# Layer 0's feed-forward in float32r halves, its transposes three tiles later, and row statistics a quad ahead

## The chip, the cores and the metric

The kernel runs on one core of a Trainium2 chip. The core has a matrix engine (PE, or TensorE) that writes into the accumulator memory PSUM, and three engines for elementwise work: DVE (VectorE), ACT (ScalarE) and POOL (GpSimd). SP only issues transfers. Each engine works through its own queue in order and waits on semaphores for the others. POOL cannot read PSUM. The metric is device time in microseconds for one execution; lower is better. An execution under the profiler gives the trace that the views below are read from.

## What is computed

The input is `x`, 8 batches of 512 rows of 256 values. Two transformer layers follow; every sub-layer normalizes its rows first and adds its result to `x`.

```python
x = x + attention0(layernorm(x))     # 16 heads of 16, causal; gamma, beta
x = x + ffn0(layernorm(x))
x = x + attention1(layernorm(x))     # 16 heads of 16, causal within 64 rows; biases, Wo
x = x + ffn1(layernorm(x))           # 256 -> 768 -> 256, int32 weights times 1/127

def fp4_linear(x, w):                # blocks of 16 along the last axis, both operands
    return fp4_quant_dequant(x) @ fp4_quant_dequant(w).T

def ffn0(y):                         # 256 -> 704 -> 256
    h = silu(fp4_linear(y, w_gate)) * fp4_linear(y, w_up)
    return fp4_linear(h, w_down)
```

`fp4_quant_dequant` divides each block of 16 by a sixth of its largest magnitude, rounds to the grid 0, 0.5, 1, 1.5, 2, 3, 4, 6 and multiplies back. So `h` has to be quantized row by row between the two matrix products of layer 0's feed-forward.

## The kernel before

The kernel has four stages, and each fills the whole core: attention 0, feed-forward 0, attention 1, feed-forward 1. A tile framework gives each tile a place and semaphores, and orders each engine's instructions by a plan made ahead; instructions that are pinned (`pin`, `keep_in_program_order`) keep the order of the code. The line numbers are those of the kernel before.

**Attention** (both layers, `attention`, L331) works in quads: four heads of one batch, two quads to a unit, 32 quads in all. `body` (L693) runs through the quads; in each it computes the maxima of the quad after next (`scores`, L436), the exponentials of this one (`Outputs`, L532) and the sums of the last one, in positions 0 to 5 (0 to 3 in layer 1), and hangs side work on these positions with `at`. Side work for batch `c + 2` is: `norm` (row statistics on DVE and POOL, then four normalizations on ACT, L742), `turned` (transposes on PE, L739), and the projections `load_q`, `load_k` (L744), whose pieces go through `store` (POOL, then SP to HBM) and come back by `fetch`. The masks are added on PE by a product of an identity (`ident_b`, bf16) with a mask that holds -1e30. `VP` holds the values of an even and an odd batch.

During attention 0 a generator, `before_ffn` (L863), is advanced at three of ten steps: it quantizes the weights of feed-forward 0 and prepares batch 0 for it. The row statistics for the other batches of feed-forward 0 also run in this stage, where the plan finds room.

**Feed-forward 0** (L976 to L1086) takes 32 row tiles of 128 rows. For tile n the code emits: `gated` (L1019), two halves of 352 columns; each half is four float32 products (gate and up, two blocks of 128 of the contraction) into one pair of PSUM banks, then SiLU on ACT (L1031) and the product with `up` on DVE (L1032) into the row tile `h`. Then quantization of `h` (`quantize`, L197): block maxima on DVE (L217), scale and reciprocal (L223 to L225), a product on POOL (L226), a magnitude on ACT (L274), two rounding steps on DVE (L276, L278), and the product with the scale on POOL (L279). Two tiles later `down` (L1034) transposes `h` in six pieces on PE (`ph`, L1041; five of 128 columns and one of 64), copies them to `hT` with three ACT copies (L1045 to L1048), and multiplies with the weights in six float32 products (`pd`, L1052). DVE adds the result to `x` (L1056). Each batch's input is prepared one batch ahead by `prepare` (L1011): normalize, quantize, transpose (`pt_f`, L853), copy to `fyT` (L858). `late_weights` (L984) brings in the weights of layer 1, and from the 27th tile on the opening of attention 1 (L666) is advanced between the tiles.

**Feed-forward 1** (L1099) already works with halves. A float32 tensor is split into `hi`, its value rounded to float32r, and `lo`, the remainder; products of float32r tiles replace one float32 product.

## Time and profile before

| What | us |
|---|---|
| Median of 3 runs (lowest 1334.25, highest 1334.98) | 1334.26 |
| The profiled execution | 1330.82 |
| Its span, first to last instruction | 1329.1 |

The stages, from the view of busy time by stretch (us):

| Stage | stretch | length | PE | DVE | ACT | POOL |
|---|---|---|---|---|---|---|
| Attention 0 | 0 to 485.6 | 485.6 | 403.2 | 387.9 | 279.7 | 249.1 |
| Feed-forward 0 | 485.6 to 807.1 | 321.5 | 300.5 | 217.1 | 113.6 | 133.1 |
| Attention 1 | 807.1 to 1171.7 | 364.6 | 335.4 | 247.0 | 176.7 | 237.9 |
| Feed-forward 1 | 1171.7 to 1329.1 | 157.4 | 146.7 | 77.9 | 80.8 | 68.5 |

A row of the timeline gives the start, the length, the engine, the line of the code, the operation, output and inputs by the program's names, the shapes, a count of merged instructions, and in brackets the idle time before it with what ended that. PEld is the loading of weights into PE, which overlaps the products. Lengths of PE rows overlap their successors, so a pace is read from start to start. A row of waits names the waiting engine and line, whom it waited for, the sum in us, the number of times and the longest. A TensorE clock of 1.00 is full speed.

### The profile page before, as it was taken

What the parts mean: (1) busy time and instruction counts of PE and PEld (TensorE: products, weight loads), DVE (VectorE), ACT (ScalarE), POOL (GpSimd) and SP (SyncE); (2) the same over time, 40 slices, a digit from 0 to 9 for tenths busy, and PEclk for the clock granted to TensorE, in tenths of its full rate; (3) what the DMA queues carried; (4) which work ended last, traced back from release to release, by engine and by line L of the source; (5) the groups of instructions that cost most, each with busy time, mean ns of one, the idle gap of its engine ahead of it and who ended that gap; (6) DMA issues with size and microseconds to landing.
All of it is one profiled execution on the core that took longest, in us unless ns stands there. A gap on an engine that the chain in (4) does not pass through costs nothing. (4 is left out here: it accounts for less than half of the span.)

```text
span 1329.1 us, 23108 instructions
## 1 busy us (share of the span) xinstructions
PE 1185.7 (89%) x8815; PEld 791.4 (60%) x8846; DVE 929.9 (70%) x1657; ACT 650.8 (49%) x1057; POOL 688.7 (52%) x912
## 2 busy tenths in 40 slices
PE   4678889889978998998999998999999999889998
PEld 2444454445534455665666666676767667668887
DVE  4699989796699847686766657676667767545553
ACT  3265655566665663332333323544455444555553
POOL 4266556464456334443443544766667566634443
PEclk9899999899989998999999999999999999999999
DMA  7643334354433310000000044454543535000001
GB/s 219 142 103 75 87 80 91 83 111 87 96 68 97 60 33 1 24 24 0 1 1 0 0 111 93 96 123 84 113 103 91 125 80 128 7 0 33 25 33 42
DMA packets 50448, 92.07 MB, mean 69 GB/s; under 512 B 6428, under 2 KB 43420, under 8 KB 44188
## 3 DMA queue, kind: packets, MB, share of 16 engines
q1 hardware_dynamic: 49452, 89.74, 29.6%
q8 instruction: 72, 1.18, 0.4%
q10 hardware_dynamic: 816, 0.79, 0.2%
q14 instruction: 44, 0.36, 0.1%
q0 software_dynamic: 64, 0.00, 0.0%
HBM read 61.15 MB, written 29.36 MB: 68 GB/s over the span
## 5 line engine op out<-in xcount | busy, mean ns | idle before, releaser
L134 POOL TENSOR_SCALAR_AFFINE_SELECT ex<-ex 128x256 f32<-128x256 f32 (+2 forms) x512 | 263.4, 525 | 230.3 <-ACT ex L575 129.9
L575 ACT ACTIVATE ex<-t 128x1024 f32<-128x1024 f32 (+1 forms) x192 | 168.0, 882 | 121.1 <-PE t L564 110.7
L469 DVE TENSOR_REDUCE mx<-s 128x2 f32<-128x1024 f32 (+2 forms) x192 | 196.6, 1035 | 39.9 <-PE s L458 30.6
L605 ACT ACTIVATE ex<-t 128x640 f32<-128x640 f32 (+1 forms) x128 | 96.8, 757 | 123.4 <-PE t L595 108.6
L635 PE MATMUL po<-ex,vp 128*32 128x128 f32 (+4 forms) x2816 | 142.9, 322 | 3.1 <-POOL ex L134 2.0
L488 DVE TENSOR_REDUCE mx<-s 128x4 f32<-128x768 f32 x128 | 121.3, 953 | 31.9 <-PE s L482 30.9
L1052 PE MATMUL pd<-wd,hT 128*128 128x256 f32 (+1 forms) x384 | 101.3, 407 | 15.9 <-ACT hT L1045 15.1
L635 PEld LDWEIGHTS po<-ex,vp 128*32 128x32 f32 x2816 | 71.2, 109 | 60.5 <-issue 31.2
L1103 POOL TENSOR_TENSOR hT<-gh,hT 128x512 fp32r<-128x512 f32 x48 | 61.7, 1291 | 82.6 <-ACT hT L1102 66.1
L453 PE MATMUL s<-kk_both,qq_both 96*128 96x512 bf16 (+3 forms) x352 | 81.9, 314 | 19.0 <-DVE mx L469 8.8
L1052 PEld LDWEIGHTS pd<-wd,hT 128*128 128x128 f32 (+1 forms) x384 | 70.1, 195 | 47.9 <-ACT hT L1045 28.0
L279 POOL TENSOR_TENSOR h<-mg_h,sc_h 128x704 f32<-128x704 bf16 x32 | 45.4, 1420 | 97.6 <-DVE mg_h L278 90.3
L1026 PE MATMUL gu<-wg,fyT 128*128 128x352 f32 x256 | 93.9, 470 | 0.0
L1026 PE MATMUL gu<-wu,fyT 128*128 128x352 f32 x256 | 86.3, 459 | 0.0
L475 PE MATMUL s<-wmask,ident_b 128*128 128x384 bf16 x256 | 83.6, 332 | 1.4 <-DVE mx L488 1.4
L564 PE MATMUL t<-qq_both,kk_both 108*128 108x512 bf16 (+3 forms) x352 | 70.4, 304 | 12.1 <-DVE mx L469 6.1
L226 POOL TENSOR_TENSOR xn_h<-h,rc_h 128x704 f32<-128x704 f32 x32 | 45.0, 1405 | 61.1 <-DVE rc_h L225 57.5
L458 PE MATMUL s<-cmask,ident_b 128*128 128x128 bf16 (+1 forms) x321 | 76.4, 238 | 0.0
L1170 DVE SCALAR_TENSOR_TENSOR gh<-ggu,gsl 128x512 f32<-128x512 f32 x48 | 33.2, 691 | 55.6 <-ACT gsl L1168 55.1
L1031 ACT ACTIVATE sl<-gu 128x352 f32<-128x352 f32 x64 | 29.4, 460 | 75.8 <-PE gu L1026 75.6
L1026 PEld LDWEIGHTS gu<-wu,fyT 128*128 128x128 f32 x256 | 48.6, 190 | 27.4 <-issue 1.0
L453 PEld LDWEIGHTS <-qq_both 96*128 96x128 bf16 x352 | 32.6, 101 | 51.5 <-issue 29.6
(256 smaller groups left out, 2661.1 us busy)
## 6 DMA issues: line engine op xcount, KB each, us to landing
q_hbm<-qp SPq DMA_DIRECT2D x96, 128.0 KB
k_hbm<-kp SPq DMA_DIRECT2D x96, 128.0 KB
qq_both<-q_hbm SPq DMA_DIRECT2D x44, 256.0 KB
kk_both<-k_hbm SPq DMA_DIRECT2D x22, 384.0 KB
qq_both<-q_hbm SPq DMA_DIRECT2D x44, 128.0 KB
kk_both<-k_hbm SPq DMA_DIRECT2D x22, 256.0 KB
qq<-q_hbm SPq DMA_DIRECT2D x20, 256.0 KB
out_dram<-go SPq DMA_DIRECT2D x16, 256.0 KB
```

Source lines behind the costliest of these rows:

```text
L134: nc.gpsimd.affine_select(out=t, in_=t, compare_op=ALU.is_ge, fill=0.0, base=base, pattern=[[0, n] for n in shape[1:-1]] + [[sign, shape[- ...
L453: pin(nc.tensor.matmul(bank[:, a * w : (a + 1) * w], lhsT=q[:KF, hs[j], t * P : w], rhs=k[:KF, hs[j], :w], start=(a == 0), stop=False, ski ...
L458: pin(nc.tensor.matmul(bank.rearrange("p (i k) -> p i k", k=w)[:, :, t * P :], lhsT=ident_b, rhs=cmask[:, : len(part), :], start=False, st ...
L469: nc.vector.tensor_reduce(dst, src, AX.X, ALU.max)
L475: pin(nc.tensor.matmul(sc[:, a, : 2 * BAND], lhsT=ident_b, rhs=mask.rearrange("p a k -> p (a k)"), start=True, stop=False,))
L488: nc.vector.tensor_reduce(mx[:, t2 : t2 + 2, js[0] : js[0] + 2].rearrange("p t j -> p j t"), sc[:, :, : 2 * BAND].rearrange("p j (t k) -> ...
L564: pin(nc.tensor.matmul(bank[:, a * w : (a + 1) * w], lhsT=k[: KF + 12, self.hs[j], t * P : (t + 1) * P], rhs=q[: KF + 12, self.hs[j], t * ...
L575: nc.scalar.activation(ex[:, :banks, :used], sc[:, :banks, :used], AF.Exp, scale=QSCALE)
L605: nc.scalar.activation(by_head[:, :, :w], sc[:, :, :w], AF.Exp, scale=QSCALE)
L635: pin(nc.tensor.matmul(self.o[HP * j : HP * (j + 1), t * P : t * P + w], lhsT=vp[:, kt, 4 * c + j, :], rhs=self.ex[kt, j][:, x0 : x0 + w], ...
L1026: nc.tensor.matmul(gu[:, i, :352], lhsT=YT[b][:, e, t * P : (t + 1) * P], rhs=w[:, e, f], start=(e == 0), stop=(e == NE - 1),)
L1052: nc.tensor.matmul(pd[:, :D], lhsT=hT[:n, k, :], rhs=wd1[:n, k, :], start=(k == 0), stop=(k == NH - 1),)
```

## The change

- *Float32r halves in feed-forward 0.* `wg1`, `wu1` and batch 0's rows are split into `HALVES` at the end of `before_ffn`; `wd1` is split where feed-forward 0 begins (one ACT copy and one POOL subtraction of 1536 columns); the rows of later batches by `split` when they are transposed (two ACT copies out of PSUM, one POOL subtraction). Each float32 product becomes three float32r products: high by high, high by low, low by high (`PAIRS`).
- *128 rows throughout.* `h` and `wd1` are padded with zeros from 704 to 768, so the sixth piece has 128 rows as the others.
- *Transposes three tiles later.* `turn_rows` transposes tile n - 3 at the head of step n, into one pair of banks, with one ACT copy for the high half and one DVE subtraction for the low half (768 columns each); `down` follows after `gated`. There is one pair of `hT` and there are four fixed row tiles `h`.
- *Quantization.* The scale uses a sixth rounded up, so the reciprocal is no longer multiplied by `DOWN` (L225 goes); the inexact form works in place, and its second rounding writes float32.
- *Statistics.* In both attentions the row statistics of batch `c + 2` move from a quad's first position in `r == 1` to the last position of `r == 0`, and the normalizations go one tile to a position.
- *Places.* The bf16 identity goes: the masks hold +1e30 and are added through the negated identity. `cmask` and the second `VP` live in the attention's own pool, and `VP` 1 is cleared in each attention. The opening of attention 1 keeps the pieces of a unit's q and k in one slot, that of `wd1`, and has one buffer for the remainder.

The diff, cut to its core:

```diff
         if not exact:
-            nc.vector.tensor_scalar(sc, am, sixth, 1e-12, ALU.mult, ALU.max)
+            nc.vector.tensor_scalar(sc, am, SIXTH_UP, 1e-12, ALU.mult, ALU.max)
             nc.vector.reciprocal(rc, sc)
-            nc.vector.tensor_scalar(rc, rc, DOWN, None, ALU.mult)
-            nc.gpsimd.tensor_tensor(blocks(xn), src, wide(rc), ALU.mult)
+            nc.gpsimd.tensor_tensor(src, src, wide(rc), ALU.mult)
...
-            nc.vector.scalar_tensor_tensor(mg, mg, MAGIC, xn, ALU.max, ALU.subtract)
-        nc.gpsimd.tensor_tensor(dst, blocks(mg), wide(sc), ALU.mult)
+            nc.vector.scalar_tensor_tensor(xn, mg, MAGIC, xn, ALU.max, ALU.subtract)
+        nc.gpsimd.tensor_tensor(dst, blocks(mg) if exact else dst, wide(sc), ALU.mult)
...
+    PAIRS = ((0, 0), (0, 1), (1, 0))
+
+    def split(pool, hi, lo, src, name):
+        n = src.free_size()
+        full = pool.tile([P, 512], F32, tag="full", name=f"full_{name}", bufs=1)[:, :n]
+        nc.scalar.copy(hi, src)
+        nc.scalar.copy(full, src)
+        nc.gpsimd.tensor_tensor(lo, full, hi.bitcast(F32), ALU.subtract)
...
+                if r == 0 and c + 2 < B:
+                    at(f3, lambda: stats(c + 2))
                 if r == 1 and c + 2 < B:
-                    at(f1, lambda: norm(c + 2))
+                    for t in range(NT):
+                        at(t, lambda t=t: norm(c + 2, [t]))
...
+            for e in range(NE):
+                nc.scalar.copy(hi[:, e], t[:, e])
+                nc.gpsimd.tensor_tensor(lo[:, e], t[:, e], hi[:, e].bitcast(F32), ALU.subtract)
+                yield
...
+        wd_halves = [
+            wp.tile([P, NH, D], F32R, tag="raw", name="wd_high"),
+            fp.tile([P, NH, D], F32R, tag="wdl", name="wd_low", bufs=1),
+        ]
+        nc.scalar.copy(wd_halves[0], wd1)
+        nc.gpsimd.tensor_tensor(
+            wd_halves[1], wd1, wd_halves[0].bitcast(F32), ALU.subtract
+        )
...
-            for i, w in enumerate((wg1, wu1)):
+            for i, w in enumerate((HALVES["wg"], HALVES["wu"])):
+                n = 0
                 for e in range(NE):
-                    nc.tensor.matmul(
-                        gu[:, i, :352], lhsT=YT[b][:, e, t * P : (t + 1) * P],
-                        rhs=w[:, e, f], start=(e == 0), stop=(e == NE - 1),
-                    )
+                    for l, r in PAIRS:
+                        nc.tensor.matmul(
+                            gu[:, i, :352], lhsT=YT[b][l][:, e, t * P : (t + 1) * P],
+                            rhs=w[r][:, e, f], start=(n == 0), stop=(n == 3 * NE - 1),
+                        )
+                        n += 1
...
+        def turn_rows(b, t):
+            h = HID.pop((b, t))
+            hT = HT[b, t] = [
+                fp.tile([P, NH, P], F32R, tag=f"hT{i}", name=f"hT{i}_{b}_{t}", bufs=1)
+                for i in range(2)
+            ]
+            pt = psum2(f"ph_{b}_{t}").rearrange("p a k -> p (a k)")
+            for k in range(NH):
+                nc.tensor.transpose(
+                    pt[:, k * P : (k + 1) * P], h[:, k * P : (k + 1) * P], ident
+                )
+            flat = [x.rearrange("p k t -> p (k t)") for x in hT]
+            nc.scalar.copy(flat[0], pt[:, : NH * P])
+            nc.vector.tensor_tensor(
+                flat[1], pt[:, : NH * P], flat[0].bitcast(F32), ALU.subtract
+            )
+
         def down(b, t):
...
+            for l, r in PAIRS:
+                for k in range(NH):
+                    nc.tensor.matmul(
+                        pd[:, :D], lhsT=hT[l][:, k, :], rhs=wd_halves[r][:, k, :],
+                        start=(l == r == k == 0), stop=(l == 1 and k == NH - 1),
+                    )
...
-        for n in range(len(tiles) + 2):
+        for n in range(len(tiles) + 3):
+            if n >= 3:
+                turn_rows(*tiles[n - 3])
             if n < len(tiles):
                 b, t = tiles[n]
-                if t == 0 and b + 1 < B:
-                    ahead = prepare(b + 1)
+                if n == 0:
+                    ahead = prepare(1)
+                    for _ in range(3):
+                        next(ahead)
+                elif t == NT - 1 and b + 2 < B:
+                    ahead = prepare(b + 2)
...
-            if n >= 2:
-                down(*tiles[n - 2])
+            if n >= 3:
+                down(*tiles[n - 3])
```

## The prediction

> **What bounds the kernel now.** I read four views in this order: busy time by stage, the busy time of one steady batch of layer 0's feed-forward, its TensorE timeline, and the waits of TensorE in the first attention. By stage (columns: stretch, its length, then busy us and instruction count of PE, weight loads, DVE, ACT and POOL, granted clock):
>
> ```profile
> 485.60:807.10 321.50, 300.54 (x1219) 200.09 (x1216) 217.14 (x385) 113.55 (x253) 133.14 (x97) 0.98 0.10 23
> ```
>
> That is the feed-forward that is rewritten, from its first matmul to the end of its last `pd`. TensorE is busy 93% of it; DVE 68%, POOL 41%. A steady batch (four row tiles):
>
> ```profile
> 671.70:709.00 37.30, 35.18 (x146) 23.58 (x145) 25.35 (x43) 13.65 (x32) 14.96 (x10) 1.00 0.00 1
> ```
>
> Its TensorE timeline (start, length, what; ends overlap the next start, so the pace is start to start):
>
> ```profile
> 671.67 3.05 PE L1052 MATMUL pd<-wd,hT 128*128 128x256 f32 x12
> 674.65 0.86 PE L1026 MATMUL gu<-wg,fyT 128*128 128x352 f32 x2
> ...
> 676.53 1.35 PE L1026 MATMUL gu<-wg,fyT 128*128 128x352 f32 x4
> 677.71 1.35 PE L1026 MATMUL gu<-wu,fyT 128*128 128x352 f32 x4
> 678.90 0.82 PE L1041 MATMUL ph<-ident,h 128*128 128x128 f32 x6
> 679.55 0.76 PE L1026 MATMUL gu<-wg,fyT 128*128 128x352 f32 x2
> ...
> 689.84 2.43 PE L1052 MATMUL pd<-wd,hT 128*128 128x256 f32 x10 [1.03 <-ACT hT L1045]
> ```
>
> A float32 product stands as two records, and four `gu` records start 1.18 us apart: 0.295 each, 16 a tile, 4.72 us. `pd` takes 2.98 (671.67 to 674.65), `ph` 0.65: 8.35 a tile, 33.4 a batch, with 0.98 for the batch's `pt_f` transposes 34.4 of 37.3. The rest is mostly the wait for the copy of `hT`, 2.1 us. So TensorE's own work bounds this stage.
>
> The price of the new form stands in layer 1's feed-forward, which already multiplies float32r halves:
>
> ```profile
> 1235.62 1.09 PE L1159 MATMUL ggu<-yT,wg_r 128*128 128x512 f32 x4
> 1236.55 1.07 PE L1159 MATMUL ggu<-yT,wu_r 128*128 128x512 f32 x4
> 1237.46 1.60 PE L1131 MATMUL gpd<-wd_r,hT 128*128 128x256 f32 x12
> 1238.89 0.40 PE L1159 MATMUL ggu<-yT,wg_r 128*128 128x512 f32 x1
> ```
>
> 512 columns cost 0.230 (four in 0.92 us), 256 cost 0.119 (twelve in 1.43).
>
> **The change, part by part.** *TensorE in the steady batch.* No row has a float32r product of 352 columns. On the line between the two rows it is 0.119 + 96/256 x 0.111 = 0.161; it can hardly be under 0.119 and not over the 0.295 of today's record. I take 0.161, since both neighbours are of the same type. `gated` becomes 24 x 0.161 = 3.86 (was 4.72), `down` 18 x 0.119 = 2.14 (was 2.98); `ph` stays 0.65. A tile is 6.65, a batch 4 x 6.65 + 0.98 = 27.6, against 34.4. The wait for `hT` goes too: in the order written out for the changed kernel, `ph` of a tile stands a whole `gated` (3.86) ahead of its `pd`, and the copy and subtraction need about 1.8.
>
> The Trainium skill, "TensorE: Matmul & The Clock Gate", section "Back-to-back issue gap", gives N/2.4 + 2.5 ns for a warm matmul. By it 352 and 256 columns cost 0.149 and 0.109 and a tile 6.19 us, 15 us less over 32 tiles; the rows above are 7 to 9% slower than the rule at 512 and 256, so I estimate by them.
>
> *DVE.* Each batch loses five L225 (454 ns x4 and 1164: 3.0 us) and gains four subtractions of 128x768 out of PSUM. The nearest rows are L1103 on DVE (512 from PSUM, 685 ns) and the 768-wide PSUM reduction L488 (953 ns): 0.95 each, 3.8. L278 writes float32 instead of bf16 at no cost: L276, which writes float32 at the same size, has the same 890 ns. 25.35 - 3.0 + 3.8 = 26.2 us.
>
> *POOL* gains two 512-wide subtractions a batch (L1103 on POOL: 1291 ns): 14.96 + 2.6 = 17.5. *ACT* swaps three copies (585, 276, 264) for one of 768 columns (about 0.8) and copies `fyT` twice: some 13.5, no bound.
>
> *What is late next.* DVE at 26.2 is nearly level with TensorE at 27.6, and two things keep DVE from running full. First, its queue waits in order for POOL and ACT: a row's reciprocal is followed by POOL's multiplication (1387), often behind another POOL row (1387), then ACT's L274 (787), and L276 stands behind that. In the steady batch these waits are 3.9 + 3.2 us; in the new order two places stay bare, the third tile's L276 (short by 1.9) and the last tile's, now queued behind `mg_x` (1.6): 3.5 us. Second, DVE and POOL do not run certain instructions at once:
>
> ```profile
> 605.54 1.39 POOL L226 TENSOR_TENSOR xn_h<-h,rc_h 128x704 f32<-128x704 f32 x1 [2.77 <-DVE rc_h L225]
> ...
> 605.82 1.16 DVE L225 TENSOR_SCALAR rc_x<-rc_x 128x64 f32<-128x64 f32 x1
> ...
> 607.12 1.93 POOL L226 TENSOR_TENSOR xn_x<-fy,rc_x 128x1024 f32<-128x1024 f32 x1 [0.19 <-DVE rc_x L225]
> ```
>
> A 64-element row takes 1.16 us, until POOL is done. L225 goes, but L276 and L278, which read two operands from SBUF, behave alike: `mg_x` takes 1917 ns here where `xn_x` of the same shape takes 1225. They are 9.6 us a batch, beside 17.5 of POOL. That sum is 27.1 in a batch meant to take 27.6. I add 2.2 us for such collisions (between nothing, if they fall into bare waits, and 7, a whole POOL row for each of five pairs). 26.2 + 3.5 + 2.2 = 32 us a batch: DVE, not TensorE, sets the new pace. What waits then is `pd`, whose third group of products needs DVE's low half of `hT`, and `ph` behind it.
>
> The Trainium skill, "GPSIMD Engine Reference", section "Key points", says that GpSimd shares its SBUF interfaces with VectorE, with contention where DVE has two SBUF inputs. It speaks against the change, which packs the same rows into a shorter batch. A sum without it is 29.7 a batch, 14 us less over six batches.
>
> *The stage.* Start: `wd_low` (1536 columns, at most 3 x 1291 = 3.9 us) stands on POOL ahead of `rs_f`, and DVE's queue holds `am_x`, `mr_f` and `rc_x` of batch 1 ahead of the first product of `h`, so that comes some 4 us later than the 491.57 of before; by the same walk the first `ph` ends 20.5 us into the stage, with three tiles through `gated`. Then six batches at 32 (192 us), 6 for layer 1's weight casts on DVE (about 10 us of work, part of it into bare waits), the last five tiles with nothing to prepare, at TensorE's pace (33.3) with the opening of attention 1 between them (14.7, from its rows), and 11.7 for the last three `pd` and two `ph`, with 4 us of waits since one pair of `hT` serves all. Sum 278 us against 321.5: **43 saved**. With batches of 27.6 and the casts hidden it is 246 (75 saved), with batches of 37 it is 308 (13 saved).
>
> *Attention 0.* One stall there is of the statistics' making:
>
> ```profile
> PE pt_a L184 <- ACT y L174: 24.5, 2, 17.9
> ```
>
> 17.9 of it is the program's start, 6.6 the wait at 366 to 372.7 us, where DVE's statistics stood late; the granted clock is 0.66 in the 7 us behind it. A quad ahead, they are done in time. I take 6 (0 to 9: DVE is full just behind, 9.91 of 10 us). Splitting the weights and batch 0's rows puts six ACT copies, the copy of `wd` (about 6 us) and six POOL subtractions (4 x 1387 + 2 x 1291 = 8.1) into the last quads; ACT is 58% and POOL 51% busy there, so I charge 2 (0 to 8).
>
> *Program start.* The bf16 identity (2.54 us on DVE) goes and POOL's `vp` memset (1.83) moves behind the masks that DVE waits for: 1.5 sooner (0 to 2.5). The mask through the negated identity is the same product: 0. `vp` 1 is cleared in each attention, 1.83 on POOL, under preparatory work that needs POOL only later: 0 (to 1.8 if not).
>
> *Attention 1.* TensorE waits 13 times for `qr`, about 1.43 us where four normalizations stand ahead on ACT and 0.94 elsewhere; tile by tile the five longer ones lose 0.5: 2 (0 to 5). SP's order of stores and fetches hardly moves, and the single slot for both pieces of a unit holds back unit 1's `q` until unit 0's stores have landed; the new order leaves TensorE some 29 us of other work there: 0 (to 5).
>
> Sum: 43 + 6 - 2 + 1.5 + 2 = 50.5. The profiled execution took 1330.82 us (span 1329.1), so 1280.3 by it. The median of the runs is 3.44 above that execution; 1334.26 - 50.5 gives **1284**.
>
> **Rivals.** *TensorE stays the bound.* DVE's waits fall beside its own backlog and the casts are hidden: 1334 - 75 - 7.5 = 1252. For it: 26.2 is below 27.6. Against: the two bare places.
> *DVE and POOL collide harder.* Batches of 37: 1334 - 13 - 7.5 = 1314. For it: three sums at 27; against: `am_h`, the products from PSUM and the reciprocal run beside POOL today.
> *Slower.* A float32r product of 352 columns takes no less than today's record, 0.295. A tile is then 24 x 0.295 + 3.04 = 10.12, the stage 32 x 10.12 + 33 (opening, tail, start) = 357, and the kernel 1334 + 35 - 7.5 = 1362. It decides from 0.259 on (32 tiles of 9.25). Against: 512 columns take 0.230.
> *The change hides its gain*: some queue I have not followed holds the stage at its old length; 1334.
>
> **How the numbers follow.** The forecast has 0.48 (about 1268 to 1300), TensorE-bound 0.23, harder collisions 0.22, slower 0.05, no gain 0.02. The range 1254 to 1312 cuts a little off both neighbours. 0.2%, 2.7 us, is about what a measurement of this kernel tells from no change: faster 0.93, same 0.02, slower 0.05.
>
> **What would show it.** In the changed profile: `gu` records 0.16 apart, `pd` 0.12; no wait of `pd` for ACT's `hT`, but waits for DVE's; DVE over 80% busy in a batch of 30 to 34 us; no stall of `pt_a` near 370. Wrong if `gu` records stand 0.26 or more apart, if a batch is near 37 us, or if DVE has idle time while `pd` never waits.

## The result, and the profile after

The changed kernel takes 1318.51 us (median of 4 executions, 1317.62 to 1320.53) against 1334.26. The record's ratio is 0.9896, with a 95% interval of 0.9872 to 0.9921 (the quotient of these two medians is 0.988). It is faster, by 15.7 us where 50 were forecast, and 6.5 us beyond the slow end of the range. By stages, from the profiled executions (each stage ends where the next one's first matmul starts):

| stage | before, us | after, us | change | forecast |
|---|---|---|---|---|
| attention 0 | 485.6 | 499.7 | +14.1 | -5.5 |
| feed-forward 0 | 321.5 | 297.4 | -24.1 | -43 |
| attention 1 | 364.6 | 364.2 | -0.4 | -2 |
| feed-forward 1 | 157.4 | 157.3 | -0.1 | 0 |

The stages sum to 10.5 us saved and not 15.7: the profiled execution of the kernel before was 3.4 us under its median, that of the changed one 2.0 over. Of the 40 us missing between these two executions, about half is in each of the first two stages. The same two stages in the view by stage (length, then busy us and instructions of PE, weight loads, DVE, ACT and POOL, granted clock), after:

```profile
0.00:499.70 499.70, 413.47 (x2993) 226.98 (x3024) 391.48 (x662) 284.46 (x402) 260.15 (x356) 0.95 0.42 91
499.70:797.10 297.40, 255.30 (x1668) 240.68 (x1665) 243.74 (x378) 117.66 (x203) 161.29 (x116) 0.95 0.11 28
```

and attention 0 before:

```profile
0.00:485.60 485.60, 403.18 (x2993) 221.31 (x3024) 387.86 (x664) 279.69 (x395) 249.12 (x349) 0.97 0.43 96
```

Attention 0 has the same 2993 records on TensorE, and they are busy 10.3 us longer: the granted clock fell from 0.97 to 0.95. Only 3.8 of its 14.1 us are more idle time. In the feed-forward, for which 278 was forecast, the clock is 0.95 where it was 0.98.

The TensorE timeline of a row tile after (start, length, what):

```profile
534.57 0.48 PE L1111 MATMUL gu<-wu_wuh,fyT 128*128 128x352 f32 x2
534.89 0.32 PE L1111 MATMUL gu<-wu_wul,fyT 128*128 128x352 f32 x1
535.05 0.32 PE L1111 MATMUL gu<-wu_wuh,fyT 128*128 128x352 f32 x1
535.21 0.87 PE L1144 MATMUL pd<-wd_high,hT 128*128 128x256 f32 x6
535.92 0.88 PE L1144 MATMUL pd<-wd_low,hT 128*128 128x256 f32 x6
536.67 0.98 PE L1144 MATMUL pd<-wd_high,hT 128*128 128x256 f32 x6
537.49 0.82 PE L1130 MATMUL ph<-ident,h 128*128 128x128 f32 x6
```

`gu` records start 0.16 apart (0.32 for two), six `pd` take 0.71 to 0.75, so 0.12 each: the prices of the new form were right to the hundredth. Two batches of four row tiles, the first with, the second without a half-clock stretch:

```profile
560.60:596.40 35.80, 30.30 (x203) 29.12 (x202) 30.29 (x47) 15.51 (x27) 21.19 (x14) 0.95 0.07 23
...
666.60:698.10 31.50, 28.43 (x202) 27.42 (x202) 28.27 (x40) 13.35 (x24) 15.68 (x11) 1.00 0.01 1
```

DVE is busy 85 and 90% of them. What TensorE waits for in the whole feed-forward (us in total, times, longest):

```profile
PE pd L1144 <- DVE hT L1135: 10.1, 8, 3.2
PE ph L1130 <- POOL h L272: 7.9, 8, 1.4
PE gu L1111 <- DVE h L1118: 5.6, 5, 2.9
PE pd L1144 <- ACT hT L1134: 5.3, 6, 2.3
```

A wait is often followed by slow matmuls. Here the last six `pd` products of a tile stand 3.15 us for the low half of `hT`, and then take 1.45 us where the six before them took 0.87:

```profile
577.21 0.87 PE L1144 MATMUL pd<-wd_low,hT 128*128 128x256 f32 x6
581.23 1.45 PE L1144 MATMUL pd<-wd_high,hT 128*128 128x256 f32 x6 [3.15 <-DVE hT L1135]
```

The trace's clock records have a stretch of 3.4 us at half speed from 581.5 on. By stage, TensorE ran at half speed for 30.7 us of attention 0 and 10.2 of the feed-forward before, and for 54.6 and 30.7 after (the clock records begin some 22 us into the program).

In attention 0 the stall near 370 us is gone, as forecast. The waits of TensorE there, after:

```profile
PE s L469 <- DVE mx L485: 17.2, 18, 3.1
PE pt_a L178 <- ACT y L168: 16.0, 1, 16.0
PE t L580 <- DVE mx L485: 11.1, 16, 1.8
PE t L580 <- ACT ex L591: 10.3, 9, 3.6
PE pot L667 <- ACT oT L660: 8.6, 6, 4.0
```

The same waits before (`pt_a` had 24.5, 17.9 of it at the start):

```profile
PE t L564 <- DVE mx L469: 13.7, 19, 2.6
PE s L453 <- DVE mx L469: 12.6, 16, 4.1
PE t L564 <- ACT ex L575: 7.3, 5, 2.4
PE pot L651 <- ACT oT L644: 1.8, 3, 0.9
```

The longest `pot` wait shows what stands in the way. ACT's timeline:

```profile
258.79 0.60 ACT L168 ACTIVATE y<-x,mr_a,rs_a 128x256 f32<-128x256 f32 x1 [3.40 <-DVE mr_a L162]
259.29 0.56 ACT L660 COPY oT<-po 128x512 f32<-128x512 f32 x1
```

and TensorE's, behind it:

```profile
259.91 0.55 PE L667 MATMUL pot<-ident,oT 128*128 128x128 f32 x3 [3.98 <-ACT oT L660]
```

A tile of the normalization stands at the head of ACT's queue and waits 3.40 us for the last step of the row statistics (`mr_a`). That step follows POOL's power (`rs_a`), which takes 1.99 us here; and it takes 1.89 us itself for four values a row, where the other seven in this stage take 0.2 to 0.6; it lasts until a quantization product on POOL is done:

```profile
254.84 1.99 POOL L160 TENSOR_TENSOR rs_a<-ve_a,mhalf 128x4 f32<-128x4 f32 x1
256.80 1.93 POOL L243 TENSOR_TENSOR pr_wu<-q_wu,sl_wu 88x1024 f32<-88x1024 bf16 x1
256.86 1.89 DVE L162 SCALAR_TENSOR_TENSOR mr_a<-mv_a,rs_a 128x4 f32<-128x4 f32 x1 [0.92 <-POOL rs_a L160]
```

The copy `oT` stands behind the normalization, and TensorE's transposes behind that. ACT's own waits for `mr_a` are not new. From 60 us to the end of the stage, before and after:

```profile
ACT y L174 <- DVE mr_a L168: 11.6, 6, 4.8
ACT y L168 <- DVE mr_a L162: 15.0, 6, 4.9
```

What changed more is what stands behind them. In order of execution the first normalization copy of a batch has moved ahead of one `oT` copy in three of these six batches, the one shown among them. The statistics are called a quad earlier, but their last step still lands just ahead of the copies that wait for it, or after them.

### The profile page after: what moved, and what is told of

Read it like the earlier page. It is cut to its first block, busy times and chain, and to the rows that moved or that the text cites. A ratio compares the mean times of both kernels' runs of the same rounds, so it can differ in the third digit from the quotient of the medians.

```text
span 1318.6 us, 24074 instructions
## 1 busy us (share of the span) xinstructions
PE 1150.1 (87%) x9263; PEld 837.3 (63%) x9294; DVE 960.9 (73%) x1648; ACT 659.0 (50%) x1014; POOL 729.8 (55%) x940
## 5 line engine op out<-in xcount | busy, mean ns | idle before, releaser
L491 PE MATMUL s<-wmask,minus_b 128*128 128x384 bf16 x256 | 83.9, 333 | 2.3 <-DVE mx L504 2.3
L272 POOL TENSOR_TENSOR h<-h,sc_h 128x704 f32<-128x704 f32 x32 | 45.9, 1434 | 68.8 <-DVE h L271 67.9
L580 PE MATMUL t<-qq_both,kk_both 108*128 108x512 bf16 (+3 forms) x352 | 71.0, 306 | 11.2 <-ACT ex L591 5.1
L474 PE MATMUL s<-cmask,minus_b 128*128 128x128 bf16 (+1 forms) x321 | 78.3, 244 | 0.0
L1144 PE MATMUL pd<-wd_high,hT 128*128 128x256 f32 x384 | 60.1, 294 | 15.6 <-DVE hT L1135 10.1
L1111 PE MATMUL gu<-wg_wgh,fyT 128*128 128x352 f32 x224 | 67.1, 341 | 2.7 <-DVE h L1118 2.7
L219 POOL TENSOR_TENSOR h<-h,rc_h 128x704 f32<-128x704 f32 x32 | 46.5, 1453 | 33.6 <-DVE rc_h L218 20.3
L1144 PEld LDWEIGHTS pd<-wd_high,hT 128*128 128x128 f32 x384 | 52.7, 197 | 19.2 <-DVE hT L1135 12.3
L267 ACT ACTIVATE mg_h<-h 128x704 bf16<-128x704 f32 x32 | 25.2, 787 | 76.4 <-POOL h L219 76.2
L1111 PE MATMUL gu<-wu_wuh,fyT 128*128 128x352 f32 x224 | 62.9, 322 | 0.0
L1259 PE MATMUL ggu<-yT,wg_r 128*128 128x512 f32 x192 | 56.4, 404 | 2.1 <-DVE yT L1203 1.1
```

The lines of the kernel that those rows point to most:

```text
L474: pin(nc.tensor.matmul(bank.rearrange("p (i k) -> p i k", k=w)[:, :, t * P :], lhsT=minus_b, rhs=cmask[:, : len(part), :], start=False, st ...
L491: pin(nc.tensor.matmul(sc[:, a, : 2 * BAND], lhsT=minus_b, rhs=mask.rearrange("p a k -> p (a k)"), start=True, stop=False,))
L580: pin(nc.tensor.matmul(bank[:, a * w : (a + 1) * w], lhsT=k[: KF + 12, self.hs[j], t * P : (t + 1) * P], rhs=q[: KF + 12, self.hs[j], t * ...
L1111: nc.tensor.matmul(gu[:, i, :352], lhsT=YT[b][l][:, e, t * P : (t + 1) * P], rhs=w[r][:, e, f], start=(n == 0), stop=(n == 3 * NE - 1),)
L1144: nc.tensor.matmul(pd[:, :D], lhsT=hT[l][:, k, :], rhs=wd_halves[r][:, k, :], start=(l == r == k == 0), stop=(l == 1 and k == NH - 1),)
```

## The experiments

The stages of all runs, in us. The ratio is to the kernel before, run beside each, with its 95% interval. The steady part is the feed-forward from the end of its first `ph` to the end of the 25th, 24 row tiles; forecast 198 (six batches of 32, and 6 for weight casts).

| kernel | median | ratio | attention 0 | feed-forward 0 (steady part) | attention 1 |
|---|---|---|---|---|---|
| before | 1334.26 | 1 | 485.6 | 321.5 | 364.6 |
| after | 1318.51 | 0.9896 (0.9872 to 0.9921) | 499.7 | 297.4 (204.3) | 364.2 |
| a_once | 1311.56 | 0.9826 (0.9797 to 0.9855) | 488.5 | 297.2 (204.6) | 367.6 |
| a_mixed | 1307.00 | 0.9806 (0.9793 to 0.9819) | 487.6 | 297.3 (204.6) | 362.8 |
| b_stats | 1339.28 | 1.0038 (1.0021 to 1.0054) | 501.1 | 319.0 | 361.8 |
| a_ahead_whole | 1324.19 | 0.9931 (0.9913 to 0.9950) | 494.4 | 295.9 (203.9) | 374.1 |
| a_stats_first | 1312.18 | 0.9855 (0.9836 to 0.9873) | 493.2 | 295.3 (203.7) | 366.0 |
| a_early | 1305.94 | 0.9801 (0.9787 to 0.9814) | 484.3 | 295.3 (203.8) | 365.7 |
| a_down_later | 1316.66 | 0.9865 (0.9815 to 0.9915) | 499.5 | 294.1 (203.9) | 363.7 |
| f_dve_more | 1319.04 | 0.9897 (0.9872 to 0.9922) | 494.0 | 298.4 (204.8) | 367.3 |
| f_pe_more | 1341.05 | 1.0078 (1.0058 to 1.0099) | 494.4 | 319.2 (223.4) | 365.6 |
| f_fix | 1312.09 | 0.9860 (0.9833 to 0.9888) | 493.6 | 292.7 (203.7) | 363.9 |
| f_no_prepare | 1276.01 | 0.9581 (0.9562 to 0.9599) | 493.4 | 260.0 (173.5) | 362.8 |
| f_spread | 1313.44 | 0.9845 (0.9821 to 0.9868) | 497.9 | 288.2 (198.3) | 366.2 |
| f_no_pool_prep | 1302.37 | 0.9773 (0.9741 to 0.9804) | 498.7 | 278.1 (188.8) | 362.8 |
| f_no_dve_prep | 1301.39 | 0.9767 (0.9735 to 0.9799) | 496.0 | 284.1 (192.7) | 361.2 |
| best | 1303.72 | 0.9794 (0.9770 to 0.9818) | 487.1 | 294.1 (204.5) | 363.4 |
| best2 | 1309.40 | 0.9814 (0.9793 to 0.9836) | 486.2 | 293.3 (203.9) | 368.0 |

In the expectations a batch is called an example. One thing to keep in mind in reading the table: after, a_down_later and the seven kernels f_ keep the changed kernel's attention 0 as it was, and it ended at 493.4 to 499.7 in these nine profiled executions (median 496.0). A difference of a few us between two single stages says little; the ratios carry the verdicts.

### Attention 0: is it the order of the statistics?

**a_once** puts the statistics and the normalization back to where they were, in both attentions, and keeps the rest:

```
-                if r == 0 and c + 2 < B:
-                    at(f3, lambda: stats(c + 2))
                 if r == 1 and c + 2 < B:
-                    for t in range(NT):
-                        at(t, lambda t=t: norm(c + 2, [t]))
+                    at(f1, lambda: norm(c + 2))
```

> The changed kernel with the row statistics and the normalization put back as they were before (in one call, all four row tiles, in the second quad of an example); everything else of the change stays. Theory S (the new order of statistics and normalization is what lengthens attention 0): attention 0 ends near 485 us instead of 499.7, with the stall near 370 back, and the kernel takes about 1304 us. Rival R (the float32r halves, the moved masks and the in-place quantization beside attention 0 lengthen it): attention 0 still ends at 499 or later, 5 to 6 us more for the stall that comes back, and the kernel takes 1318 to 1325 us.

Attention 0 ended at 488.5, with the stall near 370 back. The kernel took 1311.56 and not 1304; attention 1 came out at 367.6, 3.4 us over the changed kernel's. Theory S holds for attention 0, R falls.

**a_mixed** does the same in attention 0 alone (`if banded:` around the new form, the old one otherwise):

> The changed kernel with the old statistics and normalization in attention 0 alone; attention 1 keeps the changed order (a quad ahead, tile by tile). Nothing is left out. Theory S (the statistics' order costs in attention 0 and gains some in attention 1): attention 0 ends near 488 us, attention 1 stays at 364 to 366 instead of the 367.6 it had with both put back, the kernel takes 1307 to 1310 us. Rival (nothing in the order matters, executions scatter by where the half-clock stretches fall): 1315 to 1320, as the changed kernel.

1307.00 us, attention 0 at 487.6, attention 1 at 362.8: theory S for attention 0. That the new order gains in attention 1 is not shown: the fourteen executions that have it there as the changed kernel does range from 361.2 to 368.0, before had 364.6 and a_once 367.6, and the intervals of a_once and a_mixed overlap. Copies `oT` of a_mixed in attention 0 come 1.0 us ahead of before's in the first eight quads, 0.2 in the next fifteen, and 2.0 behind at the end. So the other parts of the change cost what was forecast for them: the start 1.0 (forecast 1.5), the splitting in the last quads 2.2 (forecast 2); 0.8 between them stays unexplained. And putting attention 0's statistics back alone takes 11.5 us off the changed kernel (1307.00 against 1318.51).

**b_stats** is the converse, the kernel before with the statistics' edit alone:

> The kernel before with the statistics' edit alone (a quad ahead, normalization tile by tile), no float32r halves in layer 0's feed-forward. Theory S: attention 0 grows by the 14 us that the changed kernel shows, attention 1 stays, the kernel takes about 1345 to 1350 us, slower than before. Rival R: the stall at 370 goes and nothing else changes, 1326 to 1330 us.

1339.28, ratio 1.0038 (1.0021 to 1.0054): slower, with attention 0 at 501.1, 15.5 us more. Its profile has the same wait as the changed kernel at the same place, ACT's view:

```profile
261.72 0.60 ACT L174 ACTIVATE y<-x,mr_a,rs_a 128x256 f32<-128x256 f32 x1 [3.38 <-DVE mr_a L168]
262.23 0.56 ACT L644 COPY oT<-po 128x512 f32<-128x512 f32 x1
```

The expected 1345 to 1350 was too high: in the profiled execution attention 1 and the feed-forward were 2.8 and 2.5 us shorter than before. Differences of this size between single stages say little.

**a_ahead_whole** keeps the statistics a quad ahead and puts the four normalization copies into one place (only the second half of a_once's diff):

> The changed kernel with the statistics still called a quad ahead, but the four tiles of a normalization in one place again (where they stood before). It tells the two halves of the statistics' edit apart. If the tile-by-tile normalization does the harm (its copies stand early in ACT's queue and exponentials wait behind them): attention 0 ends near 485 us or a little before (no stall at 370), the kernel takes 1298 to 1305 us. If calling the statistics ahead does it (DVE then works on them where it should reduce scores): attention 0 still ends near 499, the kernel takes 1315 to 1320 us. Rival R: 1315 to 1320 us as well, with the run above telling R from the second reading.

Attention 0 ended at 494.4, inside the nine executions of the full change, so calling the statistics ahead is enough for most of the harm, and what the cut by tiles adds can't be told from scatter. The kernel took 1324.19, more than the changed one though the intervals just overlap; in the profiled execution attention 1 came out at 374.1: 8 of its 10 us more are TensorE busy time, with 30.7 us at half clock there against 10.2. Why that form of attention 1 runs into it I did not follow up.

**a_stats_first** takes the statistics out of attention 0 altogether, into the opening:

```
                 land(u)
                 yield
+                if not banded:
+                    for b in ((2, 3), (4, 5, 6, 7))[u[1]]:
+                        stats(b)
...
```

(the rest keeps the results until they are used, and puts attention 0's normalization back in one place).

> The changed kernel with attention 0's row statistics of examples 2 to 7 all computed in the opening (between 20 and 40 us DVE is busy 2.8 us of 20), and attention 0's normalization in one place again; attention 1 keeps the changed order. Nothing is left out. Theory A (what the changed order costs is the chain of statistics itself: each time it runs in the middle of attention 0 among the weight quantization's DVE and POOL work, ACT stands 2 to 5 us in its queue before the first normalization copy, with oT copies and exponentials behind it): with the chain gone from there attention 0 ends at 470 to 480 us, below the 485.6 of before, and the kernel takes 1290 to 1300 us. Rival B (only the place of ACT's four normalization copies matters, which here is the old one): attention 0 ends at 485 to 490, as with the statistics put back, and the kernel takes 1305 to 1310 us.

493.2: it fell between the two, for a reason of its own. DVE ran seven chains one behind the other, each with a wait for POOL's power, and the first score product waited 11.5 us for DVE; attention 0 was 10.0 us late after its first quad and 7.6 at the end.

**a_early** mends that, with one power for a group of batches:

```
+            for i, b in enumerate(bs):
...
+                    nc.vector.bn_aggr(mv[:, i * NT + t, :], st[:, t, :])
+            nc.vector.tensor_scalar(ve, mv[:, :, 1], EPS, None, ALU.add)
...
+            nc.gpsimd.tensor_tensor(rs, ve, mhalf[:, : n * NT], ALU.pow)
+            nc.vector.scalar_tensor_tensor(mr, mv[:, :, 0], -1.0, rs, ALU.mult, ALU.mult)
```

> As the run with all statistics first, with its cost at the start mended: example 1's statistics stay ahead of the others', and those of examples 2 to 7 are worked out in two groups with one POOL power and one mean-times-scale each, so that DVE waits for POOL twice and not six times. The first wait of a score product was 11.5 us there and attention 0 was 10 us late after its first quad. Theory A: the first quad is no more than 2 us late, attention 0 ends at 482 to 486 us, the kernel takes 1300 to 1305 us. Rival: the statistics' DVE work fills no hole, the lateness only moves, and attention 0 ends at 490 or later, 1309 us or more.

1305.94, attention 0 at 484.3 (487.1 and 486.2 in the two later kernels that have it). That meets theory A's number for the stage, but barely beats the old order (487.6, 488.5), though the waits of `y` for `mr_a` are gone (but one of 9.6 us in the opening) and DVE has six batches' statistics less to do after the opening. The reason is in TensorE's waits:

```profile
PE s L469 <- DVE mx L485: 22.6, 17, 4.3
PE pt_a L178 <- ACT y L168: 15.1, 1, 15.1
PE t L580 <- DVE mx L485: 13.9, 16, 3.7
```

The products wait 36.5 us for DVE's score maxima (26.3 before). Beside the longest of them DVE's timeline has steps of the weight quantization, which now stand elsewhere. So the gain of 6 us that I had put on the stall at 370 is not to be had by this: without that stall the same time is lost at other quads (5.0 us at quad 19, 3.6 at quad 23, counted from 0).

### The feed-forward: is it DVE's pace?

**a_down_later** puts each `down` one row tile later, with two pairs of `hT`; to make room, batches of even number keep their transposed rows where batch 0's were:

```
-            if n >= 3:
-                down(*tiles[n - 3])
+            if n >= 4:
+                down(*tiles[n - 4])
```

> The changed kernel with each down product one row tile later and two pairs of hT instead of one (room for them: every second example's transposed rows lie in the buffer that held example 0's). Nothing is left out. Theory W (in the feed-forward TensorE stands in its queue before pd until DVE has the low half of hT, 15.4 us over the stage, and several of these waits are followed by 3.4 to 6.8 us at half clock): the pd waits vanish with some of the half clock, the stage drops from 297 to about 278 to 283 us and the kernel to 1299 to 1304. Rival D (DVE's queue sets the pace, 28 to 31 us busy of each batch of 32 to 36): the waits come back elsewhere (gu for h, ph for POOL's h), the stage stays within 5 us of 297 and the kernel within 5 us of 1318.

294.1, of which the steady part is 203.9: no wait of `pd` is left, and the same time stands before `ph`, `pt_f` and `gu`. Rival D's number. It gained 3 us at the end of the stage, where the last tiles have nothing behind them.

**f_dve_more** and **f_pe_more** then ask directly which engine sets the pace. The first adds to each row tile

```
+            nc.vector.tensor_reduce(
+                spare, hT[0].rearrange("p k t -> p (k t)")[:, :F1].bitcast(F32).rearrange(
+                    "p (n k) -> p n k", k=16
+                ), AX.X, ALU.max,
+            )
```

> The changed kernel with one more VectorE reduction of 704 elements (about 0.88 us, result unused) per row tile of layer 0's feed-forward, queued behind the subtraction that makes hT's low half: 28 us of DVE work in the stage. Theory D (DVE's in-order queue sets the pace of the feed-forward): the stage grows by 20 to 28 us, the kernel takes 1338 to 1347 us. Rival W (TensorE's own work and its half-clock stretches set it, DVE has room): less than 8 us more, under 1327.

the second, ahead of each `pd`,

```
+            for _ in range(4):
+                nc.tensor.matmul(
+                    pd, lhsT=wd_halves[0][:, 0, :P],
+                    rhs=wd_halves[0][:, 0:2, :].rearrange("p a k -> p (a k)"),
+                    start=True, stop=True,
+                )
```

> The changed kernel with four more float32r matmuls of 512 columns (4 x 0.23 us, result overwritten) ahead of each down product: 29 us of TensorE work in the stage, none for other engines. Theory D (DVE's queue sets the pace): most of it falls into TensorE's waits, and since these get shorter some of the half-clock stretches go; the stage grows by 0 to 10 us, the kernel takes 1318 to 1329 us. Rival W (TensorE sets the pace): 22 to 29 us more, 1341 to 1348.

The feed-forward in f_dve_more:

```profile
494.00:792.40 298.40, 255.64 (x1668) 239.25 (x1665) 259.42 (x409) 117.48 (x203) 164.18 (x115) 0.95 0.11 28
```

and in f_pe_more:

```profile
494.40:813.60 319.20, 279.16 (x1796) 258.25 (x1793) 232.51 (x380) 115.54 (x203) 161.35 (x116) 0.97 0.11 26
```

This overturned my theory D, and with it the step of the prediction that said that DVE sets the new pace. 28.0 us more of DVE work (32 reductions of 874 ns) lengthen the stage by 1.0 us; 29.4 us more of TensorE work (128 products at 0.23) lengthen it by 21.8, although the time at half clock fell from 30.7 to 20.5 us. And DVE's busy time grew by only 15.7 us for 28.0 of work, and fell by 11.2 where nothing was added but time: some 11 to 12 of its 243.7 us are not work but standing, which goes when there is something else to do meanwhile. It sits in the rounding steps of `h` (mean 1091 ns after, 974 in f_pe_more, shortest 822) and in the scale `sc_h` (463, 275 and 171 ns); without POOL's part of the preparation (f_no_pool_prep, below) these means are 917 and 334, so much of it is DVE standing beside POOL. A share of 85 to 90% busy was no sign of a full engine.

The waits of TensorE were not filled by its own additional work: it was idle 42.1 us of the stage in the changed kernel, 40.0 in f_pe_more, 42.8 in f_dve_more. I read them as waits for a chain that starts with TensorE's own products, so that they move along with it. One thing in f_pe_more speaks for caution: 5.6 of its 40.0 us stand before the added products themselves, which need a bank that DVE has still to read.

**f_fix** takes three loads off: `down` later, two buffers for the full copy in `split`, and the weight casts of layer 1 on ACT (`nc.scalar.copy(t, flat)`).

> The changed kernel with three things taken off the feed-forward's queues: each down product a row tile later with two pairs of hT (as in the run above), two buffers instead of one for the full copy that splits fyT, and layer 1's three weight casts of 1536 columns on ACT instead of DVE. Nothing is left out. Theory D: the casts alone took 4 to 5 us of DVE in the steady part, and the pt_f waits for the single buffer (2.9 us twice and 1.6) go, so the stage drops from 297 to 282 to 289 us, the kernel to 1304 to 1311 us. Rival: DVE's own products and its waits for POOL and ACT fill the room, 292 to 295 us as with the later down product alone, 1313 to 1317.

292.7: the rival's number. Again the steady part is 203.7. But for f_pe_more, every kernel up to here with the new feed-forward has it between 203.7 and 204.8.

**f_no_prepare** takes away what all of them still had, the preparation of the next batch's rows (the products use batch 1's in their place, so this part of the computation is left out):

```
-                elif t == NT - 1 and b + 2 < B:
-                    ahead = prepare(b + 2)
...
-                        gu[:, i, :352], lhsT=YT[b][l][:, e, t * P : (t + 1) * P],
+                        gu[:, i, :352], lhsT=YT[min(b, 1)][l][:, e, t * P : (t + 1) * P],
```

> The changed kernel without the preparation of the feed-forward's rows of examples 2 to 7 (no normalization, quantization, transposes and splitting of them; example 1's rows are multiplied in their place, so that part of the computation is left out). It takes away about 6 us of DVE, 7 of POOL and 1 of TensorE per batch of four row tiles. Theory B (the 26 us for which TensorE stands idle in the steady 24 tiles come from the burst of an example's preparation in the queues of ACT, DVE and POOL, two tiles of each batch; these take 8 to 12 us where the others take 6.6): the steady part falls from 204 to 165 to 172 us, the kernel to 1278 to 1288 us. Rival C (the waits come from the chain of one tile's own rows, ph for POOL and pd for hT, with or without a preparation): only TensorE's transposes go, the steady part stays at 190 us or more, the kernel at 1303 or more.

The steady part falls to 173.5 us and the kernel to 1276.01. The second half of it runs like this (the stage, then four row tiles):

```profile
493.40:753.40 260.00, 236.99 (x1620) 225.57 (x1617) 198.45 (x336) 87.43 (x149) 115.13 (x89) 0.98 0.13 32
648.60:675.10 26.50, 26.50 (x194) 26.50 (x193) 21.27 (x37) 9.64 (x16) 11.40 (x9) 1.00 0.01 2
```

Four row tiles in 26.5 us, 6.62 each with TensorE never idle at full clock: the 6.65 that I had worked out for TensorE. Theory B, if not to the number: the steady part is just over its 172, the kernel just under its 1278. Of the 30.8 us that the steady part lost, some 6 are TensorE's own transposes (six batches at 0.98) and 15.8 idle time (26.1 to 10.3); its time at half clock fell from 13.9 to 1.0 us.

**f_spread** tries to make use of it: the preparation in four pieces of 256 columns, each queued like a row of `h`.

```
+            for t in range(NT + 1):
+                if t < NT:
+                    normalize(y, X[b], st, [t])
+                    blocks = y[:, t, :].rearrange("p (n k) -> p n k", k=16)
+                    new = quantize(fp, blocks, blocks, P, 16, f"x{b}_{t}", False)
...
```

> The changed kernel with the preparation of each example's feed-forward rows (examples 2 to 7) cut by row tile: four pieces of 256 columns, one per row tile of the batch before, each queued like a row of h, in place of one piece of 1024 columns; room for it as in the run with the later down product. The same work in four times as many instructions, nothing left out. Theory P (what makes TensorE wait is the length of the preparation's instructions, 1.2 to 2.6 us each on DVE and POOL, standing in order ahead of a row's own products): the steady part falls from 204 to 180 to 190 us, the kernel to 1295 to 1304 us. Rival Q (the amount of work counts, wherever it stands, and small instructions add to it): the steady part stays at 198 to 208 us, the kernel at 1312 to 1322 us.

198.3, 6 us less than the changed kernel: the lower end of rival Q's range. And in **best2**, which adds a_early, the second buffer and the casts on ACT to it, it was 203.9:

> The run above with attention 0's statistics in two groups in the opening and its normalization in one place, two buffers for the full copy that splits fyT, and layer 1's weight casts on ACT. Nothing is left out. Theory P: attention 0 484 to 487, the steady part 176 to 188, the kernel 1278 to 1292 us. Rival Q: the kernel 1300 to 1306 us, as the version without the cut.

1309.40, ratio 0.9814, not to be told from best (0.9794, below), which doesn't have the cut but has the later `down`. So the size of the pieces is not the main thing that holds. The small instructions add to DVE's time, as two stretches of f_spread show; here it may well be full, but no run added work to this form:

```profile
550.00:585.00 35.00, 31.78 (x214) 30.55 (x213) 34.09 (x61) 14.93 (x30) 22.00 (x20) 0.95 0.07 23
585.00:620.00 35.00, 30.56 (x208) 29.69 (x208) 34.03 (x64) 15.97 (x30) 21.07 (x20) 0.95 0.08 23
```

DVE is busy 34.1 and 34.0 of 35 us.

**f_no_pool_prep** and **f_no_dve_prep** leave out one engine's share of the preparation each; `later` holds for batches 2 to 7.

```
-            nc.gpsimd.tensor_tensor(src, src, wide(rc), ALU.mult)
+            if not later:
+                nc.gpsimd.tensor_tensor(src, src, wide(rc), ALU.mult)
```

(and likewise for the last product and the splitting's subtraction), and in the other the five DVE operations of a batch, with a constant as the scale.

> The changed kernel without POOL's part in the preparation of examples 2 to 7's feed-forward rows: the two multiplications of 1024 columns are left out, and the low half of the transposed rows is a plain copy by ACT; DVE's and ACT's parts stay. It takes 6.5 us of POOL per batch away. If POOL is what holds (its long multiplications in the queue ahead of a row's own, and DVE's two-operand products standing still beside them): the steady part falls from 204 to 175 to 185 us, the kernel to 1288 to 1300 us. If DVE's part is: it stays at 196 or more, the kernel at 1310 or more.

> The changed kernel without DVE's part in that preparation: the block maxima, scales, reciprocals and both rounding products of examples 2 to 7's feed-forward rows are left out (POOL multiplies by a constant in their place, so the values are not quantized); POOL's and ACT's parts stay. It takes 5 to 6 us of DVE per batch away. If DVE's part is what holds: the steady part falls from 204 to 175 to 185 us, the kernel to 1288 to 1300 us. If POOL's is: it stays at 196 or more, the kernel at 1310 or more. If both fall by half, it is the two engines' work at the same time.

188.8 and 192.7: 15.5 and 11.6 us, together 27.1 of the 30.8 that the whole preparation is worth. Neither engine's share alone is the cause. I read it as the work of both at once, a batch's preparation on top of the rows' own; how much of that is waiting in queues and how much the two engines holding each other up, these runs do not tell apart.

**best** puts a_early's attention 0 together with f_fix's feed-forward:

> Attention 0 as in the run with the statistics in two groups in the opening, layer 0's feed-forward as in the run with the later down product, the second buffer and the casts on ACT; attention 1 as in the changed kernel. Nothing is left out. If the two parts add up: attention 0 482 to 486, feed-forward 293, attention 1 365, layer 1's feed-forward 158, the kernel 1300 us or a little less, against 1318.5 for the changed kernel. If they do not: 1305 to 1312, with the same stage times as in the single runs in one part and a longer stage in the other.

1303.72 us, ratio 0.9794 (0.9770 to 0.9818): about 14 us better than the changed kernel and 2% better than before. Nearly all of it is attention 0; a_early alone (0.9801) and a_mixed (0.9806), which is only the old order of attention 0's statistics, can't be told from it.

## Why the prediction was wrong, point by point

*The prices on TensorE were right.* 0.161 and 0.119 a record, 6.65 us a row tile: measured 0.16, 0.12, and 6.62 in f_no_prepare.

*"A quad ahead, they are done in time. I take 6."* This step failed, and it is about half of the miss. I had looked at the one stall of 6.6 us that the statistics cause in the old order, and given the new one nothing to pay. The rule that it broke: where a step is moved, look at each queue that it is moved past. With the call of the statistics the normalization's copies moved forward in ACT's in-order queue; the chain that they wait for (ten small DVE steps, POOL's power, one more DVE step) ran beside the quantization of the weights on just these two engines and did not end sooner relative to the copies. The stall itself did go: by the `oT` copies, the changed kernel is 13.6 us behind before's at quad 20 (counted from 0), gains 9.2 at quad 21, where the stall was, and ends 14.1 behind. Instead of +6 the edit is worth -11.5 us in the kernel (a_mixed) and about -5 on the kernel before (b_stats, 0.38% of 1333). That is shown. That the waits of ACT for `mr_a` are the way it happens is read from the timelines and was not tried by itself. Of the 14.1 us in the profiled execution 10.3 are products that took longer, at a lower clock, and 3.8 are idle time: what `pt_a` saved (8.5 us, with the start's part) was more than spent again at other waits.

*"DVE, not TensorE, sets the new pace", 32 us a batch.* The size was nearly right, the mechanism wrong. The steady part is 204.3 against 198, and TensorE's idle time in it 26.1 us against the 26.4 that six batches of 32 less 27.6 give. But DVE has room (f_dve_more), three quarters of more TensorE work are paid (f_pe_more), and most of the waits go with the batch's preparation (f_no_prepare: 10.3 us idle in the steady part). So that the number was near is luck. Had I looked at where in a batch the waits fall, and not only at sums per engine, it could have been seen: in the trace after, from one tile's last `ph` to the next one's, one row tile of each steady batch takes 10.5 to 12.8 us and the other three 6.6 to 8.8.

*The term that was missing: TensorE at half clock.* The feed-forward took some 19 us more than its sum of 278: 3.0 at the start, 6.3 in the steady part and 9.8 behind it. I had priced all of TensorE's work at full clock, though the view by stage gave 0.98 for before. TensorE ran at half speed for 30.7 us there. If all of that was work, it made the work 15.4 us longer (half of 30.7) than at full clock, most of the 19; that is an upper bound, since part of it falls beside waits that would be there anyway.

*"3.5 us of bare waits and 2.2 of collisions".* The collisions are there: f_dve_more shows about 12 us of DVE's busy time in the stage, 1.5 a batch in eight batches, as time that disappears when other work fills it. For that very reason they are no term to add to DVE's total, as the sum did. They can still hold up TensorE through the chain of a tile; the runs without one engine's share of the preparation fit that, without showing it apart.

*The other terms.* The start brought 1.0 to 1.9 (forecast 1.5) and the splitting cost 2.2 (2). The 2 of attention 1 can't be told from scatter (0.4 in after, 1.8 in a_mixed), and the way I gave failed: the waits of `pm` for `qr` there are 14.7 us, not less than the 14.0 of before.

*The rivals.* The total of "harder collisions", 1314, was 4.5 us from the result, but its batches of 37 were not: they take 33.8 with the casts (202.6 us for six, from the first `pd` of one batch to the next). No rival had attention 0 slower; "some queue I have not followed" in the last one, with a chance of 0.02, comes nearest, but it was said of the feed-forward.

*The signs named in advance.* `gu` 0.16 and `pd` 0.12 apart: yes. No stall near 370: yes. DVE over 80% busy in batches of 30 to 34 us: nearly (batches of 31.5 to 35.9), and misleading. No wait of `pd` for ACT's `hT`: no, 5.3 us in six waits.

## What to carry to other kernels

A busy share near 90% does not say that an engine sets the pace: add a known amount of work to it, and to its rival, and see which one the time follows. Before crediting an earlier call with the stall that it removes, find what moves forward with it in the in-order queues, and whether the chain it waits for really ends sooner beside the work that is there. And once a stage has short waits all over, expect TensorE's work to run at a lower clock in part, and leave room for it in the sum.

## What the runs showed of the hardware

*In these traces the clock changes on a fixed grid of 3.413 us, and the next window's clock goes with how busy TensorE was in the window before.* In each of the 18 profiled executions, all changes of the granted clock lie on one grid of 3.413 us (within 3 ns; in the changed kernel's, 1.228 us past each multiple of it, counted from the span's start); the grid's place against the program's start differs from execution to execution. Taking TensorE's busy share in each window of the grid:

| window at full clock, TensorE busy | windows | next window at half clock |
|---|---|---|
| under 40% | 194 | 194 |
| 40 to 55% | 211 | 124 |
| 55 to 65% | 272 | 4 |
| 65% and more | 5622 | 0 |

From half clock the way back asks for more: after 114 windows under 80% busy none returned, after 274 with 95% or more all but one did. So a wait need not be long. Of the 175 windows at full clock whose longest gap was 1.25 to 1.5 us, 61 were followed by half clock, and of the 48 with one of 2.0 to 2.25 us, 47. The Trainium skill, "TensorE: Matmul & The Clock Gate", section "HAM oscillation — how this bites in real kernels", has as its rule that no gap should be longer than about 3.4 us. By the counts above that is too lax here: much shorter gaps were followed by half clock. The free-running window of 3413 ns in the page's Part 1 agrees with the grid of these traces.

*What a microsecond at half clock costs.* 50 executions of the kernel before ran beside the experiments, the same program each time. Their spans go from 1326.1 to 1336.4 us, and their mean granted clocks from 0.969 to 0.982. With the time at half clock worked out as twice the missing clock times the span (48 to 83 us), the span follows it with a correlation of 0.91 and 0.26 us for each us. By this slope the 42 us more at half clock of the changed kernel (95.6 against 53.7 in the profiled executions) would be some 11 us; that is an estimate from the scatter between executions. A run in which only the clock differs was not tried, so how much of the miss is the clock's and how much the waits' own stays open.
